# Splitting the first image's channel statistics three to one between VectorE and ScalarE, and scaling its convolution weights on ScalarE

## The chip, the cores and the metric

The kernel runs on one core of a Trainium2 chip. A core has TensorE (PE in the profile; PEld is its loading of weights), VectorE (DVE), ScalarE (ACT), GpSimd (POOL) and SyncE (SP), which here issues nearly all DMAs. The engines run their own queues in order and wait for each other through semaphores. The metric is the device time of one execution in microseconds, as the median of several runs; a lower time is better.

## The reference

The input `x` is 4 images of 64 channels and 256 x 256 pixels, float32. Two residual blocks follow one another, each on a group-normalised input (32 groups of 2 channels per image):

```python
x = x + _L0_conv_ref(_gn(x), ...)   # 3x3 conv, gelu, 1x1 conv, depthwise taps, gelu,
                                    # top-2-of-3 experts, projection
x = x + _L1_conv_ref(_gn(x), ...)   # 3x3 conv, batch norm, relu, 3x3 conv, batch norm, relu
```

```python
def _gn(v, G=32, eps=1e-5):
    B_, C_, H_, W_ = v.shape
    g = v.reshape(B_, G, C_ // G, H_, W_)
    m = jnp.mean(g, axis=(2, 3, 4), keepdims=True)
    s = jnp.var(g, axis=(2, 3, 4), keepdims=True)
    return ((g - m) / jnp.sqrt(s + eps)).reshape(v.shape)
```

Only the mean and variance of the first image for the first `_gn` are touched by the change. Every pixel of that image has to be read before its first convolution can start, since the normalisation is folded into that convolution: its weights are multiplied by one over the standard deviation of their input channel, and the mean goes into a bias.

## The kernel before, in words

The 128 partitions hold 64 channels twice, for two sets of rows. An image is 16 chunks (`NCH`) of 8 row pairs, 1 MB each. The kernel has these stages: the opening (constants, weights, the first image's statistics), the front (the first block's convolutions, chunk by chunk, 64 units in all, with the statistics of the next image and the output of the image before interleaved), the second block's first convolution, its second convolution, and a last pass that adds and stores.

The opening, lines 979 to 1010, loads the 16 chunks of image 0 one after the other (`stats_load`, L409) into six buffers: four with tag "s" and two with tag "o". Of each chunk one half is taken by each of two engines:

- VectorE runs `bn_stats` (L414) over groups of 512 numbers, two for most chunks and four for the last, 32 in all. The results stand in the tile `st_x`, and one `bn_aggr` (L462) makes a mean and a variance of them.
- ScalarE runs two passes over 1024 numbers (`stats_piece`, L432): one adds up the values less a shift, the other their squares; each leaves one sum in `st_acc`. The shift is the mean of the first group (`stats_shift`, L419 to L424). There are 16 such pieces: two from the first chunk, one from each that follows, none from the last.

`stats_sums` (L434 to L443) turns ScalarE's sums into a mean and a variance. `combine` (L262) joins the two engines' results, n columns of `mv`, with a matmul that averages over the partitions of a group, on the means (L266) and again on the variances (L276), and ends in a Sqrt on ScalarE (L281) and a reciprocal on VectorE (L283). `scale_weights` (L445) then multiplies `u_raw`, the transformed 3x3 weights, into `us`: for image 0 in four parts on VectorE (L452), for later images in one on ScalarE (L454).

Between the chunks, the opening also prepares the input of the first unit: `x_load(0)`, on ScalarE `x_four` (L526) and `x_scaled` (L549, L551), on GpSimd `x_differences` (L532, L540) and `v_inner`, `v_outer` (L566 to L575). ScalarE's order in the opening is as written in the code. On the other engines a planner sets the order there; it puts the sums of `stats_sums` ahead of the last chunk's four groups on VectorE.

From the front on, the order of all engines is that of a written plan of steps. Per unit, PE runs `front_conv` (L492) for products (1, 2), (3, 4) and, after VectorE's "butterfly" sums (L610 to L629), products (0, 5). ScalarE copies the first two results out of PSUM (L605). GpSimd writes the tile `v` for the next unit, for which it has to wait until PE has read it.

Of the kernel before, what the change touches and what calls it, by code (L numbers as in the profile page):

```python
# [9 lines left out]
F32 = mybir.dt.float32  # L10
F32R = mybir.dt.float32r
BF16 = mybir.dt.bfloat16
AF = mybir.ActivationFunctionType
ALU = mybir.AluOpType
# [5 lines left out]
P = 128  # L20
# [7 lines left out]
NG = NPAIR // GP  # L28
# [3 lines left out]
NCH = NG // CG  # L32
# [9 lines left out]
def conv_preact_kernel(ctx: ExitStack, tc: tile.TileContext, io, col128, colset, col64):  # L42
    nc = tc.nc
# [3 lines left out]
    stat = ctx.enter_context(tc.tile_pool(name="stat", bufs=2))  # L47
# [20 lines left out]
    def flat(t):  # L68
        return t.rearrange("p a b -> p (a b)")
# [36 lines left out]
    lstat = layers.enter_context(tc.tile_pool(name="lstat", bufs=2))  # L106
# [24 lines left out]
    def c128(name):  # L131
        return m128[:, col128[name][0] : col128[name][1]]
# [129 lines left out]
    def combine(mv, n, avg, eps_t, out, name):  # L262

        mean = out[:, 0:1]
        ps = small(f"ps_m_{name}")
        nc.tensor.matmul(ps[:, 0:n], avg, mv[:, :, 0], start=True, stop=True)  # L266
        yield
        nc.vector.tensor_reduce(mean, ps[:, 0:n], AX.X, ALU.add)
        nc.vector.tensor_scalar(mean, mean, 1.0 / n, None, ALU.mult)
        d = stat.tile([P, n], F32, tag="cd", name=f"d_{name}")  # L270
        nc.vector.tensor_scalar(d, mv[:, :, 0], mean, None, ALU.subtract)
        nc.vector.tensor_tensor(d, d, d, ALU.mult)
        nc.vector.tensor_tensor(d, d, mv[:, :, 1], ALU.add)
        yield
        ps = small(f"ps_v_{name}")
        nc.tensor.matmul(ps[:, 0:n], avg, d, start=True, stop=True)  # L276
        yield
        var = stat.tile([P, 1], F32, tag="cv", name=f"var_{name}")
        nc.vector.tensor_reduce(var, ps[:, 0:n], AX.X, ALU.add)
        yield  # L280
        nc.scalar.activation(var, var, AF.Sqrt, bias=eps_t, scale=1.0 / n)  # L281
        yield
        nc.vector.reciprocal(out[:, 1:2], var)  # L283
# [113 lines left out]
    gn1, gn2, us, c1_bias = {}, {}, {}, {}  # L397
# [3 lines left out]
    st_x, st_g, x_in, shift_x = {}, {}, {}, {}  # L401
# [8 lines left out]

    def stats_group(b, g, k, i):
        if g == 0:
            st_g[b] = lstat.tile([P, NG // 2, 6], F32, tag="st_x", name=f"st_x{b}", bufs=1)
        nc.vector.bn_stats(st_g[b][:, g, :], x_in[b, k][:, i * GP : i * GP + GP, :])  # L414

    def stats_shift(b):

        first = stat.tile([P, 6], F32, tag="first", name=f"first_{b}")
        nc.vector.bn_stats(first, x_in[b, 0][:, 0:GP, :])  # L419
        mv = stat.tile([P, 2], F32, tag="first_mv", name=f"first_mv_{b}")  # L420
        nc.vector.bn_aggr(mv, first)
        shift_x[b] = stat.tile([P, 1], F32, tag="shift", name=f"shift_{b}")
        nc.vector.tensor_scalar(shift_x[b], mv[:, 0:1], -1.0, None, ALU.mult)
        st_x[b] = stat.tile([P, 2, 2 * NCH], F32, tag="st_acc", name=f"st_acc{b}")  # L424

    def stats_piece(b, n, i, at_sum=None):

        t = x_in[b, n // 2][:, n % 2 * 2 * GP : (n % 2 + 1) * 2 * GP, :]
        t = t.rearrange("p a b -> p (a b)")
        n = n if at_sum is None else at_sum  # L430
        f, bias = ((AF.Identity, shift_x[b]), (AF.Square, 0.0))[i]
        nc.scalar.activation(t, t, f, bias=bias, accum_out=st_x[b][:, i, n : n + 1])  # L432

    def stats_sums(b, mv):  # L434

        s = stat.tile([P, 2], F32, tag="st_sum", name=f"st_sum_{b}")
        n = NCH if b == 0 else 2 * NCH
        nc.vector.tensor_reduce(s, st_x.pop(b)[:, :, 0:n], AX.X, ALU.add)
        nc.vector.tensor_scalar(s, s, 1.0 / (n * 2 * GF), None, ALU.mult)
        sq = stat.tile([P, 1], F32, tag="st_sq", name=f"st_sq_{b}")  # L440
        nc.vector.tensor_tensor(sq, s[:, 0:1], s[:, 0:1], ALU.mult)
        nc.vector.tensor_tensor(mv[:, 1:2], s[:, 1:2], sq, ALU.subtract)
        nc.vector.tensor_tensor(mv[:, 0:1], s[:, 0:1], shift_x.pop(b), ALU.subtract)  # L443

    def scale_weights(b):  # L445

        us[b] = lstat.tile([P, 6, 3, C], F32, tag="us", name=f"us_{b}", bufs=1)
        parts = ((1, 3), (3, 5), (0, 1), (5, 6)) if b == 0 else ((0, 6),)
        for a, e in parts:
            o, u = (t[:, a:e].rearrange("p a b c -> p (a b c)") for t in (us[b], u_raw))  # L450
            if b == 0:
                nc.vector.tensor_scalar(o, u, gn1[b][:, 1:2], None, ALU.mult)  # L452
            else:
                nc.scalar.activation(o, u, AF.Copy, scale=gn1[b][:, 1:2])  # L454

    def stats_end(b):

        own = gn1[b] = stat.tile([P, 3], F32, tag="gn1", name=f"gn1_{b}")
        n = 2 if b == 0 else 1
        mv = stat.tile([P, n, 2], F32, tag=f"mv{n}", name=f"mv_x{b}")  # L460
        if b == 0:
            nc.vector.bn_aggr(mv[:, 1, :], flat(st_g.pop(b)))  # L462
        stats_sums(b, mv[:, 0, :])
        yield
        yield from combine(mv, n, c128("avg4"), eps, own, f"x{b}")
        if b == 0:
            scale_weights(b)
        nc.vector.tensor_tensor(gn1[b][:, 2:3], gn1[b][:, 0:1], gn1[b][:, 1:2], ALU.mult)
        yield
        ps = small(f"ps_cb_{b}")  # L470
        nc.tensor.matmul(ps[:, 0:1], both, gn1[b][:, 2:3], start=True, stop=True)
        yield
        c1_bias[b] = stat.tile([P, 1], F32, tag="c1b", name=f"c1b_{b}")
        nc.vector.scalar_tensor_tensor(c1_bias[b], ps[:, 0:1], 6.0, c128("c1_b"), ALU.mult, ALU.add)
# [505 lines left out]
    weights()  # L980
    STATS_IN = (("s", 4),) * 4 + (("o", 2),) * 2
    with tc.manual_schedule(engines={mybir.EngineType.Activation}):
        for k in range(NCH):
            stats_load(0, k, *STATS_IN[k % 6])
            if k == 0:
                stats_shift(0)
            for i in range({0: 0, NCH - 1: 4}.get(k, 2)):
                stats_group(0, 2 * k - 2 + i if k else 0, k, i)
            for n in range({0: 2, NCH - 1: 0}.get(k, 1)):
                for i in range(2):  # L990
                    stats_piece(0, 2 * k + n if k == 0 else 2 * k + 1, i, k + n if k == 0 else k + 1)
            if k == 5:
                x_load(0)
            if k == 8:
                x_four(0)
                x_differences(0)
            if k == 11:
                x_scaled(0)
                v_inner(0)
                v_outer(0)  # L1000
        x_load(1)
        x_four(1)

        first_end = stats_end(0)
        for _ in range(7):
            next(first_end)
# [338 lines left out]
    with tc.manual_schedule(  # L1345
# [8 lines left out]
        n = len(chunks)  # L1354
# [186 lines left out]
```

## Time and profile before

| What | Value |
|---|---|
| Median of 3 runs | 3026.77 us (3007.64 to 3039.1) |
| Profiled execution | 3016.92 us |
| Its span, first to last instruction | 3015.1 us |
| Mean granted TensorE clock | 0.913 |
| Busy: PE, DVE, ACT, POOL | 78%, 82%, 68%, 56% of the span |
| HBM traffic over the span | 302 GB/s |
| DMA in the first 60 us | share 0.98, 401 GB/s |
| Busy in the first 60 us: DVE, ACT, POOL, PE | 28.34, 43.01, 29.19, 3.62 us |

The times in the profile count from the start of the span. A line of the order of time gives the start, the time taken, the engine, the line of the code, the operation, what it writes and reads, how many of them follow each other, and in brackets how long the engine had been idle before it and what it waited for. `xs_in` are the chunks for the statistics, `x` those for the first convolution, `us` its scaled weights, `v` its transformed input, `ps_c` its result in PSUM and `mc` the copy of that.

### The profile page before, as it was taken

To read this page: it belongs to the slowest core of one execution; us is meant where nothing else is said; L and a number is where in the kernel's file an instruction comes from. 1 tells how busy PE (TensorE), PEld (TensorE's weight loads), DVE (VectorE), ACT (ScalarE), POOL (GpSimd) and SP (SyncE) were. 2 spreads that over 40 slices of the span, in tenths; PEclk is the share of its full clock that TensorE was granted. 3 is DMA by queue.
4 is the path that set the end of the run, shared out by engine and by line. 5 is a ranking of instruction groups with operands and counts; after the bars stand their busy time and mean duration, and the time that the engine had idled before them with its cause. 6 is when DMAs were issued, how large, how long until landed. Compare 5 with 4: busy or idle time off the path is not lost.

```text
span 3015.1 us, 52987 instructions
## 1 busy us (share of the span) xinstructions
PE 2357.4 (78%) x21576; PEld 1503.4 (50%) x21576; DVE 2478.0 (82%) x2793; ACT 2054.8 (68%) x2274; POOL 1676.3 (56%) x1210
## 2 busy tenths in 40 slices
PE   1898899998999999988999999989999999000000
PEld 1444444444544445546666667867888888000000
DVE  5678688888888999968988989979999898876665
ACT  6898887787876555557667667868888887422222
POOL 5888887776877778744445546635555555000000
PEclk9999999999999999998999999989999999555555
DMA  8565479999999879848999897746777764899999
GB/s 345 191 249 224 184 259 376 350 342 352 336 343 324 303 288 326 293 147 310 366 356 352 321 345 300 267 178 255 263 266 264 265 232 144 351 411 409 421 427 409
DMA packets 135572, 915.35 MB, mean 304 GB/s; under 512 B 14944, under 2 KB 15712, under 8 KB 40608
## 3 DMA queue, kind: packets, MB, share of 16 engines
q1 hardware_dynamic: 126112, 844.85, 75.0%
q10 hardware_dynamic: 9216, 67.11, 5.5%
q8 instruction: 169, 2.77, 0.4%
q14 instruction: 75, 0.61, 0.1%
HBM read 573.74 MB, written 338.17 MB: 302 GB/s over the span
## 4 chain that ended last, share of the span: by engine, by line
PE 28%; DMA 18%; DVE 5%; issue 2%; ACT 1%; POOL 0%; SPq 0%; DVEq 0%; ACTq 0%; POOLq 0%
PE ps_h L295 18%; PE ps_h2m L295 6%; DMA y_end<-y_d 5%; DMA h<-h_d 4%; DMA out<-h 4%; PE ps_hm L295 3%; DMA y<-in_xp 2%; DVE diff L352 1%; PE ps_o L492 1%; DMA y_d<-y 1%; DVE h L317 1%; DMA h_d<-h 1%; DMA yn<-y_d 1%; DMA xs_in<-xs_d 1%; DVE odd L361 1%
## 5 line engine op out<-in xcount | busy, mean ns | idle before, releaser
L295 PE MATMUL ps_h<-diff,w_q 128*128 128x512 f32 x3072 | 753.8, 400 | 14.3 <-DVE h L317 13.7
L295 PEld LDWEIGHTS ps_h<-diff,w_q 128*128 128x128 f32 x3072 | 576.6, 189 | 192.1 <-issue 23.7
L492 PE MATMUL ps_c<-v,us 64*64 64x256 f32 x9216 | 544.6, 385 | 42.2 <-DVE ps_c L623 36.4
L342 POOL TENSOR_TENSOR d<-yn 128x1024 f32<-128x1024 f32 x128 | 356.0, 2801 | 305.3 <-DMA yn<-y_d 188.5
L492 PEld LDWEIGHTS ps_c<-v,us 64*64 64x64 f32 x9216 | 361.3, 136 | 200.4 <-DVE ps_c L623 45.6
L342 POOL TENSOR_TENSOR d<-h 128x1024 f32<-128x1024 f32 x127 | 311.9, 2477 | 194.8 <-DVE diff L350 133.4
L492 PE MATMUL ps_a<-h,av 64*64 64x512 f32 x4080 | 386.8, 492 | 34.8 <-DVE t L686 23.9
L317 DVE SCALAR_TENSOR_TENSOR h<-ps_h,scale_w,m 128x1024 f32<-128x1024 f32 x256 | 322.8, 1279 | 76.6 <-PE ps_h L295 53.9
L540 POOL TENSOR_TENSOR x<-x 128x512 f32<-128x512 f32 x256 | 329.9, 1289 | 12.3
L1422 ACT ACTIVATE v<-y_end,shift,gn 128x2048 f32<-128x2048 f32 x64 | 133.8, 2092 | 285.1 <-DMA y_end<-y_d 249.9
L492 PEld LDWEIGHTS ps_a<-h,av 64*64 64x64 f32 x4080 | 154.2, 133 | 302.6 <-issue 195.6
L381 ACT ACTIVATE junk<-h,less_h 128x2048 bf16<-128x2048 f32 (+3 forms) x133 | 256.0, 1925 | 11.1 <-DVE h L317 11.0
L1423 DVE SCALAR_TENSOR_TENSOR h<-h,ss,v 128x2048 f32<-128x2048 f32 x64 | 149.8, 2349 | 126.1 <-ACT v L1422 102.1
L683 DVE SCALAR_TENSOR_TENSOR t<-ps_a,m,t 128x1020 f32<-128x1020 f32 x128 | 163.3, 1276 | 103.1 <-ACT t L677 101.1
L848 DVE SCALAR_TENSOR_TENSOR y<-ps_o,ob,y 128x1024 f32<-128x1024 f32 x128 | 163.7, 1279 | 80.6 <-DMA y<-in_xp 27.4
L677 ACT ACTIVATE t<-ps_a,tap_bias,m 128x1024 f32<-128x1024 f32 x128 | 154.0, 1203 | 97.5 <-PE ps_a L492 96.9
L705 ACT ACTIVATE xs<-t 128x1024 f32<-128x1024 f32 x128 | 134.9, 1054 | 116.8 <-DVE t L689 86.8
L352 DVE SCALAR_TENSOR_TENSOR diff<-d,gn,diff 128x1024 fp32r<-128x1024 f32 x128 | 208.5, 1658 | 0.3 <-ACT diff L345 0.3
L295 PE MATMUL ps_hm<-odd,w_q 128*128 128x512 f32 x768 | 194.0, 402 | 8.6 <-ACT m L311 6.0
L295 PE MATMUL ps_h2m<-odd,w_q 128*128 128x512 f32 x768 | 193.2, 400 | 8.2 <-DVE odd L361 4.4
L345 ACT ACTIVATE diff<-d 128x1024 fp32r<-128x1024 f32 x128 | 135.1, 1055 | 83.4 <-POOL d L342 82.2
L532 POOL TENSOR_TENSOR x<-x,x 128x512 f32<-128x512 f32 x128 | 160.7, 1278 | 43.3 <-ACT x L526 43.3
(226 smaller groups left out, 4306.5 us busy)
## 6 DMA issues: line engine op xcount, KB each, us to landing
x<-in_xc SPq DMA_DIRECT2D x64, 1280.0 KB
h<-h_d SPq DMA_DIRECT2D x64, 1152.0 KB
yn<-y_d SPq DMA_DIRECT2D x60, 1152.0 KB
xs_in<-in_xp SPq DMA_DIRECT2D x64, 1024.0 KB
xs_d<-xs SPq DMA_DIRECT2D x128, 512.0 KB
xs_in<-xs_d SPq DMA_DIRECT2D x64, 1024.0 KB
y<-in_xp SPq DMA_DIRECT2D x64, 1024.0 KB
y_d<-y SPq DMA_DIRECT2D x64, 1024.0 KB
```

The source lines that it names most:

```text
L295: nc.tensor.matmul(ps, wq[w][:, kind, kx, :], t[:, rows, kx : kx + W], start=(j == 0), stop=(j == len(terms) - 1))
L317: nc.vector.scalar_tensor_tensor(h.rearrange("p (e k) w -> p e (k w)", e=2), ps.rearrange("p e k w -> p e (k w)"), w_scale[w], m.unsqueeze ...
L342: engine.tensor_tensor(raw.rearrange("p (g r) w -> p g r w", g=2), *pair, ALU.subtract)
L352: nc.vector.scalar_tensor_tensor(lower, raw, scale, upper.bitcast(F32), ALU.mult, ALU.subtract)
L381: nc.scalar.activation(junk[rows, 0:n], flat(h), AF.Square, bias=less[name][rows], accum_out=total)
L492: last[:] = [nc.tensor.matmul(ps[o, at_out[0] : at_out[1], :], w[i], rhs[i], **flags)]
L532: nc.gpsimd.tensor_tensor(x4[:, j - 1], x_rows(u, j + 2), x4[:, j - 1], ALU.subtract)
L540: nc.gpsimd.tensor_tensor(x[:, r : r + 2], x[:, r + 2 : r + 4], x[:, r : r + 2], ALU.subtract)
L677: nc.scalar.activation(flat(t), flat(ps), AF.Identity, bias=tap_bias, scale=sh[:, 1:2])
L683: nc.vector.scalar_tensor_tensor(t[:, :, 1:W], ps[:, :, 0 : W - 1], sh[:, 0:1], t[:, :, 1:W], ALU.mult, ALU.add)
L848: nc.vector.scalar_tensor_tensor(y, ps.rearrange("p x s w -> p x (s w)"), out_bias[b], y, ALU.add, ALU.add)
L1423: nc.vector.scalar_tensor_tensor(h, h, ss2[:, 0:1], v, ALU.mult, ALU.add)
```

## The change

The split of image 0 becomes three quarters to one. Even chunks, and the last one, go wholly to VectorE (four groups each, no ScalarE piece). Odd chunks and the last but one go to both, two groups and one piece each. That makes 48 groups and 8 pieces. The groups' results are aggregated in three parts of 16 groups, each as soon as its groups are there (`stats_join`). With ScalarE's sums that gives four columns of mean and variance, which `combine` joins instead of two; `mv`, the tile for them, is now made at the start (`stats_open`). The shift for ScalarE's sums still comes from the first group of chunk 0.

The order in which ScalarE meets `x_four(0)` and `x_scaled(0)` in the code is kept: after the statistics of chunks 8 and 11.

`scale_weights` runs on ScalarE for image 0 too, still in four parts, of 384, 384, 192 and 192 numbers for each partition. Nothing else is changed.

```diff
     def stats_group(b, g, k, i):
         if g == 0:
-            st_g[b] = lstat.tile([P, NG // 2, 6], F32, tag="st_x", name=f"st_x{b}", bufs=1)
+            st_g[b] = lstat.tile([P, 3 * NG // 4, 6], F32, tag="st_x", name=f"st_x{b}", bufs=1)
         nc.vector.bn_stats(st_g[b][:, g, :], x_in[b, k][:, i * GP : i * GP + GP, :])
+
+    def stats_join(b, i):
+        n = NG // 4
+        nc.vector.bn_aggr(mv_x[b][:, 1 + i, :], flat(st_g[b][:, i * n : i * n + n, :]))
+
+    mv_x = {}
...
-        n = NCH if b == 0 else 2 * NCH
+        n = NCH // 2 if b == 0 else 2 * NCH
...
-            if b == 0:
-                nc.vector.tensor_scalar(o, u, gn1[b][:, 1:2], None, ALU.mult)
-            else:
-                nc.scalar.activation(o, u, AF.Copy, scale=gn1[b][:, 1:2])
+            nc.scalar.activation(o, u, AF.Copy, scale=gn1[b][:, 1:2])
+
+    def stats_open(b):
+        n = 4 if b == 0 else 1
+        mv_x[b] = stat.tile([P, n, 2], F32, tag=f"mv{n}", name=f"mv_x{b}")
 
     def stats_end(b):
 
         own = gn1[b] = stat.tile([P, 3], F32, tag="gn1", name=f"gn1_{b}")
-        n = 2 if b == 0 else 1
-        mv = stat.tile([P, n, 2], F32, tag=f"mv{n}", name=f"mv_x{b}")
-        if b == 0:
-            nc.vector.bn_aggr(mv[:, 1, :], flat(st_g.pop(b)))
+        n = 4 if b == 0 else 1
+        if b > 0:
+            stats_open(b)
+        mv = mv_x.pop(b)
         stats_sums(b, mv[:, 0, :])
...
     with tc.manual_schedule(engines={mybir.EngineType.Activation}):
+        stats_open(0)
+        groups = pieces = 0
         for k in range(NCH):
             stats_load(0, k, *STATS_IN[k % 6])
             if k == 0:
                 stats_shift(0)
-            for i in range({0: 0, NCH - 1: 4}.get(k, 2)):
-                stats_group(0, 2 * k - 2 + i if k else 0, k, i)
-            for n in range({0: 2, NCH - 1: 0}.get(k, 1)):
+            both_engines = k % 2 == 1 and k < NCH - 1 or k == NCH - 2
+            for i in range(2 if both_engines else 4):
+                stats_group(0, groups, k, i)
+                groups += 1
+                if groups % (NG // 4) == 0:
+                    stats_join(0, groups // (NG // 4) - 1)
+            if both_engines:
                 for i in range(2):
-                    stats_piece(0, 2 * k + n if k == 0 else 2 * k + 1, i, k + n if k == 0 else k + 1)
+                    stats_piece(0, 2 * k + 1, i, pieces)
+                pieces += 1
```

## The prediction

> **What bounds the kernel now.** I read the page's forty slices first, to see what share the changed stretch has, then the order of time of DVE, ACT and POOL from 46 to 69 us, then who waited for whom there. The change touches only work that ends before the first convolution; in the slices that is less than the first one (75 us each). The page:
>
> ```profile
> PE   1898899998999999988999999989999999000000
> DVE  5678688888888999968988989979999898876665
> ACT  6898887787876555557667667868888887422222
> ```
>
> PE is idle in the first slice and busy after it: the opening is a delay ahead of a long PE-paced body, so what it saves can at best move everything behind it, once. What ends the statistics (columns: start us, us, engine, line, operation, and the idle time before with its releaser):
>
> ```profile
> 46.83 1.28 DVE L414 BATCH_NORM_STATS2 st_x<-xs_in 128x6 f32<-128x512 f32 x2 [1.19 <-DMA xs_in<-in_xp]
> 52.93 0.18 DVE L438 TENSOR_REDUCE st_sum<-st_acc 128x2 f32<-128x32 f32 x1 [4.82 <-ACT xs_in L432]
> 53.63 2.46 DVE L414 BATCH_NORM_STATS2 st_x<-xs_in 128x6 f32<-128x512 f32 x4
> 56.12 1.02 DVE L462 BATCH_NORM_AGGREGATE mv_x<-st_x 128x2 f32<-128x192 f32 x1
> ```
>
> VectorE starts on chunk 14 the moment its load lands (46.83), and chunk 15 lands one load pitch later (2.48 us, the distance of the starts before: 44.36, 46.83), about 49.31. But the sums of ScalarE's half stand in VectorE's queue ahead of chunk 15's groups and wait until 52.93 for ScalarE, which is behind: its pieces are 2.31 us apart and it has 16 of them beside the work on the first convolution's input. So the opening is bound by ScalarE, 4 us beyond the load. Behind the statistics:
>
> ```profile
> 59.73 0.29 ACT L281 ACTIVATE var_x<-var_x,eps 128x1 f32<-128x1 f32 x1 [4.58 <-DVE var_x L279]
> 60.33 3.48 DVE L452 TENSOR_SCALAR us<-u_raw,gn 128x384 f32<-128x384 f32 x1
> 63.95 4.30 PE L492 MATMUL ps_c<-v,us 64*64 64x256 f32 x48 [4.45 <-DVE us L452]
> 62.33 5.41 POOL L540 TENSOR_TENSOR x<-x 128x512 f32<-128x512 f32 x4
> 68.31 0.60 ACT L605 ACTIVATE mc<-ps_c 128x512 f32<-128x512 f32 x1 [8.29 <-PE ps_c L492]
> 72.01 0.69 DVE L617 TENSOR_TENSOR d<-mc,ps_c 128x512 f32<-128x512 f32 x1 [1.58 <-ACT mc L605]
> 75.02 10.76 PE L492 MATMUL ps_c<-v,us 64*64 64x256 f32 x144 [3.71 <-DVE ps_c L623]
> ```
>
> The first scaled weights take 3.48 us, and PE waits 4.45 us for them. These lines are the whole path that the change can shorten.
>
> **What the Trainium skill says.** "SBUF — State Buffer", Who interferes with whom: a tensor_scalar in a two-port mode shares a port pair with GpSimd and the loser blocks fully, while ScalarE has its own ports. The trace agrees: the 128x384 scaling took 3.48 us beside GpSimd's running pair (59.89 to 62.37), and the cheapest of the four scalings was 0.31 us. "ScalarE: Activation LUTs", What ACT_TABLE_LOAD costs: an ACTIVATE with one pointer operand takes about 0.28 us + 0.833 ns an element, overlapping the next by 0.093; the trace's same instruction on later images (128x1152) took 1.241 us, where this gives 1.24. The same page, Table sets: plain copies are in every set; in the trace copies run after Sqrt without a load. No page prices the statistics instructions; the trace does.
>
> **The change part by part.**
>
> *Statistics moved.* ScalarE loses 8 of 16 pieces: 8 x 2.31 = 18.5 us. VectorE gains 16 groups at 0.645 (1.29 for two) = 10.3 us, and its one aggregate over 192 numbers becomes three over 96 (ScalarE's sums are the fourth part). An aggregate took 0.18 us for 6 numbers and 1.02 for 192; on a line, 96 cost 0.59 (bounds 0.18 and 1.02). Two of the three lie inside the stream. Its cover: VectorE idles 18.9 us for these loads. Per two chunks it now needs 6 x 0.645 + 0.16 = 4.0 us in a pitch of 4.96, so it stays load-bound; after an even chunk (4 groups, 2.46, plus an aggregate) it is up to 0.6 us late and recovers in the odd one. Without that cover some 11 us would be on the path.
>
> *Loads.* The order on SP is unchanged. Buffers of even chunks now wait for VectorE alone. Chunk 0 comes free near 13.5 instead of 16.09; the DMA share is 1.0 from 10 us on, so earlier issues gain nothing, and the load of x chunk 1 still lands near 49.31 + 3.1 = 52.4.
>
> *GpSimd's preparation of chunk 0.* Its ScalarE step (34.46) now follows piece 7, which ends near 31.0, so GpSimd starts 3.5 us earlier and the step that halted ScalarE at 44.25 is ready near 40.8. It no longer delays pieces 13 and 14.
>
> *End of the statistics.* The last piece starts when chunk 14 lands, 46.83, and takes 2.41 as now (50.50 to 52.91): 49.24. Sums 0.70: 49.96; chunk 15 has landed; four groups 2.49: 52.45; last aggregate 0.59: 53.04 against 57.14. **Gain 4.1 us** (3.7 to 4.5 by the aggregate's bounds).
>
> *Joining four parts.* Same instructions on 4 columns instead of 2: from aggregate to Sqrt 2.59 us as now, so Sqrt at 55.6. Its table load sits behind the input step of x chunk 1: that runs now from 52.81, so its end is 53.85 at the latest and the load ends by 55.15. It stays hidden by 0.45 us at least; what is late next is this load, not ScalarE's pieces. Reciprocal 0.49 later: 56.1.
>
> *Scaling on ScalarE.* First part 0.28 + 0.833 x 0.384 = 0.60 us against 3.48; the rest at 0.51, 0.35 and 0.35 pitch, hidden under the first 4.30 us of matmuls. PE can start at 56.12 + 0.06 + 0.60 + 0.1 = 56.9 against 63.95: 7.05 earlier. VectorE's product at L468, which stood behind the scalings until 67.76, is free at once. Queued behind the scalings on ScalarE is only the first PSUM copy, which waits for PE to 61.2 anyway.
>
> *What is late next.* GpSimd starts its share of the second chunk when the mean is known: 4.1 earlier, and its four L540 steps end at 67.74 - 4.1 = 63.65. ScalarE's queue is: PSUM copy (61.2), two scalings of x that need those steps, then the second PSUM copy. The scalings start at 63.65 and, as now (68.81 to 70.52), the copy can follow 1.7 later: 65.35 to 65.95, against 71.38 to 71.98. VectorE's L617 then starts at 66.0 instead of 72.01, and PE's next block at 69.0 instead of 75.02. So of 7.05 the shift keeps **6.0 us**; GpSimd's next wait (77.96, for that block) moves with it.
>
> *Carry.* Apart from the moved statistics and scalings, and the waits attached to them, all five engines run the same instructions in the same order to the end, and the later loads are issued on release. I let the shift stand: profiled execution 3016.92 - 6.0 = **3010.9**. That execution is 9.9 us below the median shown; on the median, 3026.77 - 6.0 = **3020.8**.
>
> **Rivals.**
> 1. *Only GpSimd's or a later wait counts:* the first chunk's gain is eaten and 0 to 3 us remain (a colder PE after a gap of 5.0 instead of 3.7 us: 48 matmuls took 4.30 at first and 2.82 after, so 1.5 lost per cold start; or a later alignment of loads). For: GpSimd is 98% busy from 60 to 70 us, and the shift there is only 4.1. Against: that block runs slow now as well (144 in 10.76). About 3025.
> 2. *Slower: VectorE becomes the pace of the loads.* If each group cost more in the fuller stream, buffers come free late and the load stretches. It decides where a group's mean passes (4.96 - 0.16)/6 = 0.80 us for the stream, and turns the sign where the statistics end about 2.9 us beyond 57.14 (scaling on ScalarE gives 2.9 back): (60.0 - 10.2 - 2.5)/49 = 0.97 us. At double price, 1.29, the end is 10.2 + 63.2 + 2.5 = 75.9 and the kernel is about 16 us slower: 3043. Against: groups ran 0.673 to 0.696 us throughout, also beside GpSimd's work from 35.6 to 50.6 us.
> 3. *A larger gain, 8 to 12 us:* the earlier start moves the first slots of the next image's statistics into idle ScalarE time. Little speaks for it; 3017.
> 4. *The change doesn't do what it says:* scaling on ScalarE needs a further table load and its wait. One load is 1.28 us; the order of instructions has none there. 3022.
>
> **How the numbers follow.** Forecast 0.66, rival 1 0.19, rival 2 0.05, rival 3 0.07, rival 4 0.03. All but a strong form of rival 2 lie within 1% (30 us), about what a measurement of this kernel can tell from no change; the three runs before alone spread from 3007.64 to 3039.1. The cases' own width is 3017 to 3027, but the measured time also has that spread (19 below, 12 above the median), so the range is 3003 to 3035. Faster by over 1%: 0.05, slower: 0.03, both mostly the spread; within: 0.92.
>
> **What would show it.** Right: the sums at VectorE's L444 start near 49.3, the last aggregate ends near 53.0, Sqrt near 55.6, four scalings on ScalarE with about 0.60 and 0.44 us, first convolution matmul near 56.9, the block now at 75.02 near 69.0, and conv blocks hundreds of us later still some 6 us earlier. Wrong: group means above 0.80 us, gaps in DMA before 50 us, the table load ending after VectorE's variance, PE's block at 75.02 moved by less than 4, or a lead that shrinks through the later stages.

## The result and the profile after

The changed kernel takes 3009.78 us (median of 22 runs, 3000.82 to 3017.61), the kernel before, in runs beside it, 3018.41 us (22 runs, 3007.64 to 3039.10). The ratio is 0.9971, with a 95% interval of 0.9961 to 0.9982: between 5.4 and 11.8 us less. Two further sets of runs of the same changed kernel gave 0.9982 [0.9972, 0.9992] and 0.9982 [0.9970, 0.9993]. The mean of the three is 0.9978, or 6.5 us. The profiled execution took 3004.01 us, its span 3002.2 us, at a mean TensorE clock of 0.914.

The forty slices of the changed kernel's page:

```profile
PE   2888899998999999988999999989999999100000
DVE  6678688888888899978998889969999898876665
ACT  4898887787876555557667667868888888432222
```

The first slice now has PE busy for over two tenths, where it had one. From the second slice on the picture is that of before: the body is still PE's.

The order of time of the changed kernel around the end of the statistics (columns as before: start us, us, engine, line, operation, and the idle time before with its releaser):

```profile
46.84 1.29 DVE L414 BATCH_NORM_STATS2 st_x<-xs_in 128x6 f32<-128x512 f32 x2 [1.21 <-DMA xs_in<-in_xp]
49.34 0.17 DVE L444 TENSOR_REDUCE st_sum<-st_acc 128x2 f32<-128x16 f32 x1 [1.22 <-ACT xs_in L438]
50.02 2.46 DVE L414 BATCH_NORM_STATS2 st_x<-xs_in 128x6 f32<-128x512 f32 x4
52.52 0.59 DVE L418 BATCH_NORM_AGGREGATE mv_x<-st_x 128x2 f32<-128x96 f32 x1
53.49 1.28 ACT L281 ACT_TABLE_LOAD   x1
55.70 0.29 ACT L281 ACTIVATE var_x<-var_x,eps 128x1 f32<-128x1 f32 x1 [0.93 <-DVE var_x L279]
```

Chunk 14 is met at the same instant as before (46.84 against 46.83), so the loads have not moved. The sums start at 49.34 instead of 52.93, since ScalarE no longer trails; they waited 1.22 us for it, not 4.82. The last aggregate takes 0.59 us instead of 1.02 and ends at 53.11, not 57.14. The table load for the Sqrt ends 0.93 us before the Sqrt can start.

The same view behind the statistics:

```profile
56.23 3.35 DVE L475 TENSOR_TENSOR gn<-gn 128x1 f32<-128x1 f32 x1
56.23 1.81 ACT L457 ACTIVATE us<-u_raw,gn 128x384 f32<-128x384 f32 x4 [0.23 <-DVE gn L283]
56.99 4.61 PE L499 MATMUL ps_c<-v,us 64*64 64x256 f32 x48 [1.52 <-ACT us L457]
58.30 5.31 POOL L547 TENSOR_TENSOR x<-x 128x512 f32<-128x512 f32 x4
61.66 0.60 ACT L612 ACTIVATE mc<-ps_c 128x512 f32<-128x512 f32 x1 [3.61 <-PE ps_c L499]
62.29 0.63 ACT L556 ACTIVATE e<-x 128x512 f32<-128x512 f32 x1
62.96 1.06 ACT L558 ACTIVATE x<-x 128x1024 f32<-128x1024 f32 x1
64.72 0.60 ACT L612 ACTIVATE mc<-ps_c 128x512 f32<-128x512 f32 x1 [0.71 <-PE ps_c L499]
65.35 0.69 DVE L624 TENSOR_TENSOR d<-mc,ps_c 128x512 f32<-128x512 f32 x1 [1.58 <-ACT mc L612]
68.36 10.91 PE L499 MATMUL ps_c<-v,us 64*64 64x256 f32 x144 [3.71 <-DVE ps_c L630]
```

All four scalings take 1.81 us on ScalarE, and PE starts at 56.99 instead of 63.95. The block of 144 matmuls (products 0 and 5, the mark of the prediction) starts at 68.36 instead of 75.02: 6.66 us earlier. Two lines are not as forecast: the product at L475 (L468 before) takes 3.35 us, and the scaling of `x` at L556 starts at 62.29, while GpSimd's four steps at L547 last until 63.61.

The opening of the changed kernel in groups of like instructions (count, busy us, mean ns, idle before and its releasers), VectorE in the first 57 us and then ScalarE in the first 60:

```profile
L414 DVE BATCH_NORM_STATS2 st_x<-xs_in 128x6 f32<-128x512 f32 x48 | 29.7, 677 | 9.3 <-DMA xs_in<-in_xp 9.3
L418 DVE BATCH_NORM_AGGREGATE mv_x<-st_x 128x2 f32<-128x96 f32 x3 | 1.8, 584 | 0.1
```

```profile
L438 ACT ACTIVATE xs_in<-xs_in,shift 128x1024 f32<-128x1024 f32 x8 | 9.2, 1148 | 15.3 <-DVE st_x L414 8.9 <-DMA xs_in<-in_xp 6.3
L457 ACT ACTIVATE us<-u_raw,gn 128x384 f32<-128x384 f32 x2 | 1.1, 608 | 0.2 <-DVE gn L283 0.2
L457 ACT ACTIVATE us<-u_raw,gn 128x192 f32<-128x192 f32 x2 | 0.8, 442 | 0.0
```

VectorE still waits 9.3 us for loads, so it remains load-bound with 48 groups at 0.677 us. ScalarE's pieces wait 8.9 us for VectorE, which nobody feels. The scalings took 0.608 and 0.442 us.

To follow the 6.66 us further, I compared the start of the same GpSimd instruction in two traces, here against the first profile of before (us, negative is earlier; columns are times in that profile, the last is GpSimd's next instruction after 2501 us, near the end):

```
                     100     180     220     400     800    1200    2000    2500    3014
after              -6.64   -6.65   -6.66   -8.52   -7.26   -5.93   -7.81   -7.79  -12.91
after_again        -5.48   -5.51   -4.00   -5.25   -0.05   +0.03   +0.45   +0.40   -5.07
after_third        -6.98   -5.34   -3.85   -5.73   -5.12   -4.51   -9.77   -9.69  -11.62
before_again       +0.96   +0.95   +2.45   +3.05   +4.48   +5.25   +2.18   +2.16   -3.37
```

The first row alone reads like a gain that grows from 6.7 to 12.9 us. The other rows say how it must be read. Two executions of one program drift apart on the way: before_again lies up to 7.2 us behind the first profile of before (at 1500 us), and after_again and after_third stand 10.2 us apart at 2000 us. All four rows drop by 1.9 to 5.5 us behind 2501 us, before_again too: the first profile of before was long there, in a part that the change doesn't touch. The growth from 6.66 to 8.52 us between 220 and 400 us goes with the granted clock: it falls to half for 3.41 us at 271.8 and again at 333.2 us in the first profile of before, and not at all between 231 and 398 us in that of the changed kernel.

### The profile page after: what moved, and what is told of

Its sections match the earlier page's. It is cut to its first block, busy times and chain, and to the rows that moved or that the text cites. A ratio compares the mean times of both kernels' runs of the same rounds, so it can differ in the third digit from the quotient of the medians.

```text
span 3002.2 us, 52969 instructions
## 1 busy us (share of the span) xinstructions
PE 2358.1 (79%) x21576; PEld 1501.7 (50%) x21576; DVE 2475.2 (82%) x2807; ACT 2039.1 (68%) x2246; POOL 1668.6 (56%) x1210
## 4 chain that ended last, share of the span: by engine, by line
PE 28%; DMA 18%; DVE 5%; issue 2%; ACT 1%; POOL 0%; SPq 0%; DVEq 0%; ACTq 0%; POOLq 0%
PE ps_h L295 18%; PE ps_h2m L295 6%; DMA y_end<-y_d 5%; DMA h<-h_d 4%; DMA out<-h 3%; PE ps_hm L295 3%; DMA y<-in_xp 2%; DMA y_d<-y 2%; DMA xs_in<-xs_d 1%; DVE diff L352 1%; PE ps_o L499 1%; DVE h L317 1%; DMA yn<-y_d 1%; DVE h L1437 1%; DMA h_d<-h 1%
## 5 line engine op out<-in xcount | busy, mean ns | idle before, releaser
L295 PE MATMUL ps_h<-diff,w_q 128*128 128x512 f32 x3072 | 755.5, 400 | 11.8 <-DVE h L317 11.5
L342 POOL TENSOR_TENSOR d<-yn 128x1024 f32<-128x1024 f32 x128 | 348.8, 2744 | 310.7 <-DMA yn<-y_d 176.4
L547 POOL TENSOR_TENSOR x<-x 128x512 f32<-128x512 f32 x256 | 329.9, 1289 | 12.4
L352 DVE SCALAR_TENSOR_TENSOR diff<-d,gn,diff 128x1024 fp32r<-128x1024 f32 x128 | 200.2, 1594 | 0.3 <-ACT diff L345 0.3
L539 POOL TENSOR_TENSOR x<-x,x 128x512 f32<-128x512 f32 x128 | 160.7, 1278 | 40.9 <-ACT x L533 40.9
```

The costliest lines, as they stand in the source:

```text
L295: nc.tensor.matmul(ps, wq[w][:, kind, kx, :], t[:, rows, kx : kx + W], start=(j == 0), stop=(j == len(terms) - 1))
L342: engine.tensor_tensor(raw.rearrange("p (g r) w -> p g r w", g=2), *pair, ALU.subtract)
L352: nc.vector.scalar_tensor_tensor(lower, raw, scale, upper.bitcast(F32), ALU.mult, ALU.subtract)
L539: nc.gpsimd.tensor_tensor(x4[:, j - 1], x_rows(u, j + 2), x4[:, j - 1], ALU.subtract)
L547: nc.gpsimd.tensor_tensor(x[:, r : r + 2], x[:, r + 2 : r + 4], x[:, r : r + 2], ALU.subtract)
```

## The experiments

Each kernel ran in five rounds beside the kernel before. The shifts are starts of the block of 144, against 75.02 in the first profile of before; the first 48 matmuls are those of products 1 and 2.

| Run | first 48 take, us | block starts, us | shift, us | ratio to before, 95% interval |
|---|---|---|---|---|
| before_again | 5.40 | 76.04 | +1.02 | 1.0010 [0.9996, 1.0023] |
| after | 4.61 | 68.36 | -6.66 | 0.9971 [0.9961, 0.9982] |
| after_again | 5.40 | 69.60 | -5.42 | 0.9982 [0.9972, 0.9992] |
| after_third | 4.23 | 68.07 | -6.95 | 0.9982 [0.9970, 0.9993] |
| stats_only | 4.47 | 71.00 | -4.02 | 0.9999 [0.9986, 1.0011] |
| scale_only | 5.40 | 72.99 | -2.03 | 0.9995 [0.9984, 1.0006] |
| all_vector | 5.12 | 68.52 | -6.50 | 0.9984 [0.9968, 0.9999] |
| sums_early | 4.12 | 68.63 | -6.39 | 0.9979 [0.9964, 0.9995] |
| groups_twice | 4.46 | 84.77 | +9.75 | 1.0013 [1.0003, 1.0024] |
| groups_thrice | 5.40 | 114.45 | +39.43 | 1.0115 [1.0091, 1.0140] |
| warm_pe | 2.82 | 67.39 | -7.63 | 0.9956 [0.9945, 0.9968] |
| warm_again | 2.83 | 67.41 | -7.61 | 0.9962 [0.9952, 0.9973] |
| warm_early | 4.85 | 68.33 | -6.69 | 0.9973 [0.9958, 0.9988] |

**Each half alone.** stats_only is the changed kernel with the scaling back on VectorE; scale_only is the kernel before with nothing but the scaling on ScalarE.

```diff
 stats_only, against the changed kernel
-            nc.scalar.activation(o, u, AF.Copy, scale=gn1[b][:, 1:2])
+            if b == 0:
+                nc.vector.tensor_scalar(o, u, gn1[b][:, 1:2], None, ALU.mult)
+            else:
+                nc.scalar.activation(o, u, AF.Copy, scale=gn1[b][:, 1:2])
```

> The three-to-one split of the statistics alone; the first image's weights are scaled on VectorE as before. Theory (two separate terms, 4.1 us for the statistics and 2.9 for the scaling): the last aggregate ends near 53.1 us as with the whole change (57.1 before), the first scaling on VectorE takes about 3.5 us again, PE's first convolution matmul starts near 59.9 (63.95 before), its block after the butterfly near 71.0 (75.02 before), and the kernel is about 4 us faster than before (ratio 0.9987). Rival (GpSimd, or a later wait, hides the statistics' gain and only the scaling counts): the block stays within 1 us of 75.0 and the ratio is 1.000.

> The scaling on ScalarE alone; the statistics stay split half and half. Theory: the last aggregate ends near 57.1 us, Sqrt near 59.7, the first scaling takes 0.61 us instead of 3.48, PE's first convolution matmul starts near 61.0 (63.95 before), the block after the butterfly near 72.3, and the kernel is about 2.7 us faster than before (ratio 0.9991). Rival (GpSimd, whose share of the second chunk doesn't move here, binds at once): the block starts within 1 us of 75.0, ratio 1.000.

In the order of time, stats_only first, then scale_only:

```profile
52.36 0.59 DVE L418 BATCH_NORM_AGGREGATE mv_x<-st_x 128x2 f32<-128x96 f32 x1
56.14 6.28 DVE L458 TENSOR_SCALAR us<-u_raw,gn 128x384 f32<-128x384 f32 x4
59.75 4.47 PE L502 MATMUL ps_c<-v,us 64*64 64x256 f32 x48 [4.45 <-DVE us L458]
71.00 10.84 PE L502 MATMUL ps_c<-v,us 64*64 64x256 f32 x144 [3.71 <-DVE ps_c L633]
```

```profile
55.91 1.02 DVE L459 BATCH_NORM_AGGREGATE mv_x<-st_x 128x2 f32<-128x192 f32 x1
60.03 1.82 ACT L451 ACTIVATE us<-u_raw,gn 128x384 f32<-128x384 f32 x4 [0.23 <-DVE gn L283]
60.79 5.40 PE L489 MATMUL ps_c<-v,us 64*64 64x256 f32 x48 [1.52 <-ACT us L451]
72.99 9.69 PE L489 MATMUL ps_c<-v,us 64*64 64x256 f32 x144 [3.71 <-DVE ps_c L620]
```

On VectorE the four scalings take 6.28 us in all and PE again waits 4.45 us for the first, as before; on ScalarE PE waits 1.52 us. So each half takes out its own wait and leaves the other's. The first 48 matmuls took 4.30 to 5.40 us in these profiles, which no edit explains (the runs with a warm TensorE, below, do); taking that duration off the block's start (75.02 - 4.30 = 70.72 for before, 70.64 for before_again) leaves what the edits did: stats_only 66.53, 4.1 to 4.2 earlier; scale_only 67.59, 3.1 earlier; the whole change 63.75, 64.20 and 63.84 in its three profiles, 6.4 to 7.0 earlier. The halves add up to 7.2 or 7.3 us, so at most 0.9 us of one is lost to the other. The times of the halves are too close to no change for a verdict: stats_only's interval ends at 4.2 us less, scale_only's at 4.8 us less. (The medians of the same set, 3013.27 and 3015.82 us beside 3016.93 for before, would give 3.7 and 1.1 us less. That each half is worth its shift in the time of the whole is not shown.)

**Is ScalarE needed at all?** all_vector computes all 64 groups on VectorE, none on ScalarE.

```diff
-            st_g[b] = lstat.tile([P, 3 * NG // 4, 6], F32, tag="st_x", name=f"st_x{b}", bufs=1)
+            st_g[b] = lstat.tile([P, NG, 6], F32, tag="st_x", name=f"st_x{b}", bufs=1)
...
-            for i in range(2 if both_engines else 4):
+            for i in range(4):
...
```

> All 64 groups of the first image's statistics on VectorE in four parts, none on ScalarE, no shift and no sums; scaling on ScalarE as in the change. Theory: VectorE needs 2.46 us a chunk and 0.59 for each of four aggregates against a pitch of 2.48; it falls back by about 1.1 us behind the last chunks, saves the wait for ScalarE and the 0.7 of sums, and the last aggregate ends at 53.0 to 53.6 us: within 0.6 us of the change, so the same time (ratio 0.997 to the kernel before). Rival (a fuller VectorE stretches the loads through late buffers): the last chunks land more than 1 us later than 49.3, the aggregate ends after 55, and the kernel loses 2 us or more of the gain.

```profile
L414 DVE BATCH_NORM_STATS2 st_x<-xs_in 128x6 f32<-128x512 f32 x64 | 38.3, 673 | 1.5 <-DMA xs_in<-in_xp 1.5
```

That group line of VectorE's first 60 us shows 1.5 us of waiting for loads left of 9.3: VectorE alone is about as fast as the loads. Its last aggregate ended at 52.75, a little before the 53.0 to 53.6 expected and 0.36 earlier than in the changed kernel, in which the sums stand ahead of the last groups. The block came at 68.52, or 63.40 without the first 48; its ratio cannot be told from the changed kernel's. The gain doesn't need a balance of three to one; it needs ScalarE out of the end.

**Sums off the end.** sums_early gives ScalarE chunk 6 instead of chunk 14, so that its sums could be done before the last chunk lands.

```diff
-            both_engines = k % 2 == 1 and k < NCH - 1 or k == NCH - 2
+            both_engines = k % 2 == 1 and k < NCH - 1 or k == 6
```

> As the change, but ScalarE's eighth piece comes from chunk 6 instead of chunk 14, so that its sums are done before the last two chunks. Theory (the end of the statistics now hangs on ScalarE's last piece and the 0.7 us of sums in VectorE's queue): the last aggregate ends near 52.4 instead of 53.1, set by chunk 15's landing at 49.3, the table load (54.8) still ends ahead of Sqrt's input (55.0), the block starts near 67.7 instead of 68.4; ratio as of the change within the measurement. Rival (the table load, late by the load of the second x chunk, takes the place of the wait): Sqrt stays at 55.7 and the block at 68.4.

```profile
46.95 0.17 DVE L444 TENSOR_REDUCE st_sum<-st_acc 128x2 f32<-128x16 f32 x1 [1.23 <-ACT xs_in L438]
47.15 0.94 DVE L445 TENSOR_SCALAR st_sum<-st_sum 128x2 f32<-128x2 f32 x1
48.40 4.84 DVE L414 BATCH_NORM_STATS2 st_x<-xs_in 128x6 f32<-128x512 f32 x8
53.27 0.59 DVE L418 BATCH_NORM_AGGREGATE mv_x<-st_x 128x2 f32<-128x96 f32 x1
```

A miss: 52.4 was expected, and the last aggregate ended at 53.86, later than in the changed kernel. The sums stand ahead of chunk 14's groups now; behind them eight groups run back to back, so that VectorE, not the load, ends last, and what the sums take is on the path. The wait of 1.23 us ahead of them costs little: it ends at 46.95, and in the changed kernel chunk 14 was met at 46.84. But the sums took 1.45 us, from 46.95 to 48.40, and not 0.7 as in the changed kernel, because the scaling of two numbers at L445 took 0.94 us instead of 0.17: it ran beside a GpSimd instruction that ended at 48.06, and ended at 48.09. In the changed kernel the wait of 1.22 us, which ends at 49.34, costs next to nothing too, if chunk 15 lands one pitch behind chunk 14, near 49.32; what costs is the sums' own 0.7 us. In both places that were tried the sums' duration is on the path, and in the changed kernel it is the shorter one.

**The cost of a group, and a late opening.** groups_twice computes each group once more into a tile that nothing reads; groups_thrice twice more.

```diff
         nc.vector.bn_stats(st_g[b][:, g, :], x_in[b, k][:, i * GP : i * GP + GP, :])
+        again = lstat.tile([P, 6], F32, tag="again", name=f"again_{b}_{g}", bufs=2)
+        nc.vector.bn_stats(again, x_in[b, k][:, i * GP : i * GP + GP, :])
```

> The whole change, and every statistics group of the first image is taken twice on VectorE, the second time into a scratch tile that nobody reads. It prices VectorE's cover. Theory: 12 groups for two chunks need about 7.4 us against a load pitch of 4.97, so VectorE becomes the pace of the loads; 97 groups of 0.60 to 0.62 us after 9.96, with sums and aggregates, put the last aggregate near 71 to 73 us instead of 53.1, and the delay of about 18 to 20 us is carried whole to the end: ratio to the kernel before near 1.0035 (about 10 us slower), 19 us slower than the changed kernel. Rival (the opening's length is absorbed by later waits): the last aggregate moves but the total is within 4 us of the changed kernel, ratio near 0.998.

> The changed kernel with every group of the first image's statistics computed three times (two results unread), a pure delay at the end of the opening that is large beside the scatter of the times. Groups ran 0.593 us apart back to back, so 48 more add 28.5 us to the opening of groups_twice: last aggregate ends near 97.7, the block of 144 starts near 113.2, 37 to 38.5 us later than before. Theory (every us at the opening is carried to the end): 3054 to 3056 us, ratio 1.0122 to 1.0130. Rival (the stages behind take up part of it; groups_twice showed only 4 of its 9.75 us in its ratio): +12 to +20 us, ratio 1.004 to 1.0066. In between: part of it is taken up, and the trace shows where the lag shrinks.

In the order of time of groups_twice, and then of groups_thrice:

```profile
45.05 0.67 DVE L416 BATCH_NORM_STATS2 again<-xs_in 128x6 f32<-128x512 f32 x1
45.64 0.67 DVE L414 BATCH_NORM_STATS2 st_x<-xs_in 128x6 f32<-128x512 f32 x1
...
72.78 0.16 DVE L477 TENSOR_TENSOR gn<-gn 128x1 f32<-128x1 f32 x1
73.54 4.46 PE L501 MATMUL ps_c<-v,us 64*64 64x256 f32 x48 [1.52 <-ACT us L459]
```

```profile
98.16 0.59 PE L266 MATMUL ps_m_x<-mv_x,m 128*128 128x4 f32 x2 [88.22 <-DVE mv_x L452]
101.98 5.40 PE L502 MATMUL ps_c<-v,us 64*64 64x256 f32 x48 [1.52 <-ACT us L460]
```

Groups start 0.59 us apart although each is shown with 0.67: neighbours overlap. VectorE now paces the loads, as rival 2 has it, and the opening is longer by as much as 48 further groups take (28.4 us between the two kernels). In groups_twice the last aggregate ends at 69.2 us, a little before the 71 to 73 expected. Does such a shift reach the end? groups_thrice was made to tell that apart: its block starts 39.4 us late (38.4 against before_again), its GpSimd instructions are 41.2 us late at 2000 us, and the ratio says 34.7 us, with an interval of 27.4 to 42.2. Carried whole (37 to 39 us) lies inside it, the rival's 12 to 20 us does not; that up to some 10 us of it are taken up is not excluded. groups_twice does not fit: its ratio says 0.9 to 7.2 us, and 9.75 lies outside. Its lag against the first profile of before did shrink from 9.9 us at 800 to 3.9 at 2000, but two executions of one program differ by as much. So most of a long shift reaches the end; that shifts of under 10 us are kept whole is not shown by these runs.

**The change again, and before again.**

> The kernel before, once more, as a measure of what one profiled execution and one comparison can tell. Theory (the opening's shift is fixed by the program, and the lead wanders later with short drops of the granted TensorE clock and with the load pass at the end): the marks of the opening come within 0.3 us of the first profile (last aggregate 57.1, block 75.0), the time of the same instructions further on differs from the first profile by up to 5 us either way, and the ratio is 1.000 within 0.0015. Rival (the order of instructions fixes the time everywhere, so the lead of 7.8 us at 2000 us and of 12.9 at the end in the changed kernel is the change's own): two profiles of this kernel agree within 1 us up to the end.

> The changed kernel, once more. Theory (a shift of 6 to 7 us carried to the end): the block after the butterfly within 0.5 us of 68.4, a lead of 6.6 us over the kernel before at 150 us, later leads anywhere between 2 and 11, and a ratio of 0.9978 plus or minus 0.001. Rival (the change gains more later, 8 to 12 us): ratio 0.9965 or less again, and a lead that grows in the same place (260 to 350 us) as in the first profile.

> The changed kernel, a third set of runs, beside the next two. Theory (the shift of 6 to 7 us at the opening is carried whole, the rest is wander between executions): last aggregate ends at 53.0 to 53.9, first 48 matmuls take anything from 4.1 to 5.4 us, the block of 144 starts at 68.3 to 69.6, ratio to the kernel before 0.9975 to 0.9982 (-5.4 to -7.5 us). If part of the shift were lost later: ratio above 0.9990.

after_again lost 5.8 us of its lead in one place, near 415 to 421 us: PE waited there for VectorE's tap sums (L693) for 6.5 us in 40, with 2.6 in the like stretch of the first profile, at a mean granted clock of 0.91 (it is at half from 414.7 to 421.5 us). A smaller step stands in most profiles, of about 1.5 us between 180 and 220 us (in the table above: both later rows of the changed kernel, and before_again). The stretch in windows (columns: length, PE, PEld, DVE, ACT and POOL busy with their counts, granted clock, DMA share, GB/s), first `after`, then after_again, and within after_again the part that makes its mean clock 0.96:

```profile
180.00:220.00 40.00, 35.95 (x552) 19.07 (x548) 29.70 (x36) 38.68 (x57) 35.05 (x34) 1.00 0.66 251
```

```profile
180.00:220.00 40.00, 35.94 (x528) 18.55 (x516) 28.99 (x34) 37.27 (x56) 33.48 (x32) 0.96 0.63 235
192.90:196.20 3.30, 3.30 (x40) 1.99 (x36) 3.23 (x3) 2.02 (x4) 2.24 (x2) 0.50 0.00 0
```

The 0.96 is no slightly lower clock: for 3.41 us, from 192.9 us on, the granted clock is at half, and at 1.0 around it. PE is busy for as long over the 40 us and does fewer matmuls (528 for 552), and ScalarE gets 1.4 us less work. The two first profiles have no such drop there, before_again and after_third have one: it is no effect of the change.

**TensorE warm at the start.** warm_pe adds 19 matmuls whose result nothing reads to the changed kernel: ten of 256 columns on chunk 14 when it has landed, nine of 128 beside the matmul on the variances. warm_early adds the same nineteen on chunk 8, from 31.8 us on, some 15 us earlier.

```diff
+    def warm(rhs, n, name):
+        ps = bank("a", name)
+        for j in range(n):
+            nc.tensor.matmul(ps[:, 0, 0, 0 : rhs.shape[1]], both, rhs, start=True, stop=True)
...
         x_four(1)
+        warm(x_in[0, NCH - 2][:, 0, :], 10, "ps_warm_0")
...
         at_slot(0, 0, x_load, 2)
+        at_slot(0, 0.01, warm, x_in[0, NCH - 2][:, 0, 0:P], 9, "ps_warm_1")
```

> As the change, with 19 matmuls whose result nobody reads put on PE between the landing of chunk 14 and the first convolution, so that PE isn't cold. Theory (behind PE's first 4.6 us GpSimd's third step on the second chunk, ending at 62.3, is the next limit): the first 48 matmuls take 2.8 to 3.1 us instead of 4.6, ScalarE's first PSUM copy comes near 60.0 instead of 61.7, but the scaling of x still waits to 62.3, so the second copy moves from 64.7 to 64.0 at most and the block from 68.4 to 67.7. Rival (PE's cold start alone is the limit): the block moves by the whole 1.7 us, to 66.7. If the extra matmuls hold up the variance matmul, all marks come up to 0.5 us later.

> The same as warm_pe, a second set of runs. Its first set gave 0.9956, some 13 us under the kernel before, while its block of 144 started only 7.6 us earlier than in the first profile of before. Theory (only the shift at the opening counts, the rest was scatter): first 48 matmuls at 2.8 us again, block near 67.4, ratio 0.9970 to 0.9976 (-7.2 to -9 us). Rival (the warm matmuls do something further, worth 4 to 6 us, behind the opening): ratio at or below 0.9960 again, and below that of warm_early by 0.0015 or more.

> The changed kernel with the same nineteen added matmuls, but on the data of chunk 8, some 20 us before the convolution, where TensorE falls idle again after them. Theory (what helps in warm_pe is that TensorE is busy right ahead of the first convolution): first 48 matmuls take 4.1 to 5.4 us as without them, block at 68.3 to 69.6, ratio as the changed kernel's, 0.9975 to 0.9982. Rival (the added matmuls help through the program's layout or by any activity of TensorE): first 48 matmuls under 3.5 us, or a ratio of 0.9965 or less.

In the order of time of warm_pe:

```profile
46.99 5.93 PE L989 MATMUL ps_warm<-xs_in,both 128*128 128x256 f32 x20 [37.02 <-DMA xs_in<-in_xp]
54.96 1.14 PE L989 MATMUL ps_warm<-xs_in,both 128*128 128x128 f32 x8
56.62 2.82 PE L499 MATMUL ps_c<-v,us 64*64 64x256 f32 x48 [0.52 <-ACT us L457]
59.50 0.60 ACT L612 ACTIVATE mc<-ps_c 128x512 f32<-128x512 f32 x1 [1.83 <-PE ps_c L499]
62.14 0.63 ACT L556 ACTIVATE e<-x 128x512 f32<-128x512 f32 x1 [2.05 <-POOL x L547]
63.77 0.58 ACT L612 ACTIVATE mc<-ps_c 128x512 f32<-128x512 f32 x1
```

and of warm_early:

```profile
56.70 4.85 PE L499 MATMUL ps_c<-v,us 64*64 64x256 f32 x48 [1.52 <-ACT us L457]
```

The granted clock of the first convolution (windows as above), in warm_pe and then in warm_early:

```profile
56.60:66.80 10.20, 5.96 (x98) 4.09 (x98) 6.61 (x8) 4.70 (x8) 9.96 (x9) 1.00 0.79 330
```

```profile
56.70:60.80 4.10, 4.10 (x40) 2.78 (x44) 2.60 (x1) 1.05 (x3) 3.94 (x5) 0.50 1.00 421
```

The first 48 matmuls take 2.82 us, in warm_again 2.83, about as the second 48 do (2.82 to 2.91); with the same matmuls 15 us earlier they take 4.85. So what costs 1.3 to 2.6 us at the start is that PE comes to it idle, and the traces show what the idle time does: the granted clock is at a half. In warm_early it rose to 1.0 after the added matmuls, fell to a half at 43.8 us and rose again at 60.9, 4.2 us after the first matmul of the convolution. In the twelve profiles with an idle PE the rise comes 2.7 (sums_early) to 6.1 us (groups_thrice) after that first matmul; up to it, four matmuls start 0.43 us apart, behind it 0.22. Where it comes later than 5.4 us, all 48 run slowly: those are the four profiles with 5.40. With PE faster, the chain behind it is the one that the prediction had put there: ScalarE's scaling of `x` waits 2.05 us for GpSimd, and the second PSUM copy follows 1.6 us later. That caps the gain at this block: it starts 0.7 to 2.2 us earlier than in the changed kernel's three profiles.

The times show more. warm_pe and warm_again take 3006.43 and 3005.38 us, beside 3011.68 and 3010.40 for the changed kernel on the same chips: about 5 us less each time, where the block gives 1.3 on the mean. But warm_early, on the same chip as warm_again and with a slow start, has a median of 3005.96 us, as low as warm_again's, and its ratio, 0.9973, has an interval that holds both the changed kernel's ratio and warm_again's. At 2000 us the two traces lead the first profile of before by 5.4 and 7.9 us, no more than two of the changed kernel's three do (7.8, 9.8, and 0.4 behind). The rival of a further effect behind the opening asked for a ratio of at most 0.9960 and 0.0015 between it and warm_early; 0.9962 and 0.0011 came out, and the theory's 0.9970 to 0.9976 overlaps with one of the two intervals only at its edge. Where the other 3 to 4 us come from stays open; warm_early's median speaks against a warm start as their cause without deciding it, and its rival, that the added matmuls act in some other way, is not ruled out. By the ratio warm_pe and warm_again are the lowest of the kernels run.

## Why the prediction was right

The forecast was 6.0 us less and a ratio within 1%. Three sets of runs give 6.5 us on the mean, with intervals that together reach from 2.1 to 11.8 us. The time itself was forecast at 3020.8 us and came at 3009.78: of the 11.0 us between them 8.4 come from the starting point, the median of three runs (3026.77), which was that much above the median of 22 (3018.41). The range held it because it was made wide for this spread. That 6.0 is so near to the 6.66 us of the block and to the 6.5 of the ratios is in part luck: a term of about 1 us was taken off for a wait that did not occur, and the start of the block scatters by 1.5 us in one program. By its steps:

- **Statistics moved, end of the statistics.** Forecast: sums at 49.24, last aggregate ended at 53.04. Measured: 49.34 and 53.11, a gain of 4.0 us for 4.1; stats_only, which does this part alone, ends them at 52.95. GpSimd's preparation of chunk 0 came 2.6 us earlier (33.01 for 35.58) and not 3.5, and nothing waited for it. The straight line between two aggregates was good to the hundredth (0.59), and VectorE kept its cover: 9.3 us of its waits for loads remain. The price in rival 2 was the one that was off: at double price it put the end at 75.9, groups_twice had its statistics by 69.7, because I had counted half of a pair's time (0.645) for each group, where starts are 0.593 apart. Its mechanism did come, and made the kernel slower.
- **Joining and table load.** Forecast: Sqrt at 55.6, the load hidden by 0.45 us at least. Measured: 55.70, hidden by 0.93. Rival 4 is out: between the Sqrt and the scalings there is no load.
- **Scaling on ScalarE.** Forecast: 0.60 us for the first part, PE at 56.9. Measured: 0.61 and 56.99. The Trainium skill, "ScalarE: Activation LUTs", What ACT_TABLE_LOAD costs, from which the price came, agrees also for 192 numbers: 0.44 from it, 0.442 in the trace.
- **The product "free at once": wrong.** It took 3.35 us, from 56.23 to 59.58, beside GpSimd's two steps at L539 and the first at L547, which ended at 59.56; so it did with the scaling on ScalarE in the old split (3.36 in scale_only). In groups_twice, where GpSimd had done these steps before, it took 0.16. The Trainium skill, "SBUF — State Buffer", Who interferes with whom, has the rule that I had passed over: a VectorE instruction with two SBUF inputs contends with a GpSimd instruction that reads SBUF. The slot beside GpSimd that the scaling left was not free for the next of VectorE's instructions. It cost nothing, since PE needs the product at 61.5 us only.
- **What is late next: right chain, one link mis-sized.** I let ScalarE's scaling of `x` wait for all four steps of GpSimd (63.65). It needs three, which end near 62.2, as warm_pe shows by waiting for the third until 62.14. In the changed kernel it came behind the first copy, at 62.29, when the third step had just ended (62.26), and so waited for nothing; the second copy waited for PE (64.72 instead of 65.35), and the block came at 68.36 instead of 69.0. So the term of 7.05 - 6.0 = 1.05 us that I took off was 6.96 - 6.66 = 0.30, and that is the slower first 48 matmuls (4.61 for 4.30), not GpSimd. GpSimd holds the second copy only where PE starts warm.
- **The duration of the first 48 matmuls.** I took 4.30 us as fixed. It is anything from 4.12 to 5.40, so that the block starts between 68.07 and 69.60 in one and the same program. The Trainium skill, "TensorE: Matmul & The Clock Gate", Part 1: The HAM clock gate, states that the warm-up of about 3.4 us varies from run to run, because the window that watches TensorE runs freely. The traces agree with a window of that length, since every stretch at half the granted clock between 60 and 700 us lasts 3.41 or 6.83 us, and with a start that varies. The warm-up itself was 2.7 to 6.1 us here, and that is the figure to use for this kernel; the runs with TensorE busy ahead of the convolution (2.82 and 2.83) agree with the cause. Of rival 1's reasons, this one is real, at up to 1.1 us.
- **Carry.** Not shown for a shift of this size. The three ratios, 6.5 us on the mean, agree with it, and groups_thrice carried 34.7 [27.4, 42.2] of some 39 us; groups_twice, with 0.9 to 7.2 of 9.75 us, does not agree. In single profiles the drift between two executions of one program, up to 10 us, hides it. That the first pair of profiles showed 12.9 us at the end and not 6.0 is that drift and the long tail of the first profile of before.

Rival 3 (8 to 12 us) had 0.07. The first ratio, 0.9971, would have allowed it; the two later sets and the block's shift speak against it.

## What to carry to other kernels

Where a load's end is followed by an engine that trails it, count what is queued between the last byte and the first consumer, and give the trailing share to whoever idles for the load; how the shares are balanced mattered little here, who stands last mattered by 4 us. A gain at the start of an engine-paced body is worth at most one shift, and its size is read at the first block that every engine depends on, not at the end of one pair of profiles: run the same program twice before reading a drift. If TensorE comes out of a long wait, matmuls that keep it busy right up to the first that counts (19 here) take its slow start off the path; the same 19 done some 15 us before it did not.

## What the runs showed of the hardware that was not expected

The slow start of TensorE differs by execution: 48 matmuls of 64x256 took 4.12, 4.23, 4.30, 4.46, 4.47, 4.61, 4.85, 5.12 or 5.40 us after an idle time and 2.82 or 2.83 behind 19 others. In the traces this is the moment at which the granted clock rises from 0.5 to 1.0, 2.7 to 6.1 us after the first matmul. It seems to decide more than the start: the drop of the granted clock to a half for 3.41 us, near 190 to 199 us (198 in groups_thrice, without its delay), is missing in just the four profiles whose first 48 matmuls took 4.30 to 4.61 us (before, after, stats_only, groups_twice), and stands in the other ten. That is a coincidence in fourteen traces, not a test. One such drop is worth 1.5 us, and a mean clock of 0.96 over 40 us is all that a coarse window shows of it.

A product of 128x1 numbers with both inputs in SBUF took 3.35 us beside GpSimd and 0.16 us without. It met the first of two GpSimd instructions at L539, which ended at 57.11, and ended only behind the third that followed on it, at 59.58. A scaling of two numbers in sums_early (L445) took 0.94 us beside GpSimd for 0.17.
